# Other waves of token lists, and a re-drawn order, in a two-layer attention and expert kernel

## The chip, the cores and the metric

One core of a Trainium2 chip runs the whole program. The metric is the device time of one execution in microseconds; of several runs the median is taken. The engines are named as in the profile: PE is TensorE (PEld its weight loads), DVE is VectorE, ACT is ScalarE, POOL is GpSimd and SP is SyncE, whose queue issues most of the DMAs.

## What is computed

16 sequences of 256 tokens of 128 numbers (4096 tokens, all float32) pass two layers. Each layer is an attention, then a mixture of eight experts, each followed by a layer norm of input plus output:

```
x = layernorm(x + attention0(rmsnorm(x)))      # 16 heads of 64, softmax over 256 keys
x = layernorm(x + shared(x) + sum of the 2 best of 8 experts, by their softmax weight)   # hidden 256
x = layernorm(x + attention1(x))               # see below
x = layernorm(x + sum of the 2 best of 8 experts, by weight)                             # hidden 512
```

The experts' gelu is exact. The second attention has 16 heads of 8 and goes, as the reference writes it, over the heads of one token ("bnhd,bngd->bnhg"): each token has a 16 by 16 table of scores of its own, so it is elementwise work, not a matrix product over tokens.

## The kernel before, in words

**Tiling.** Tokens lie in 8 groups of 512, each four chunks of 128 tokens (one per partition). A unit of layer 0's attention is one sequence and two heads: 128 units, numbered in the order in which `attention0` (L662) takes them. For a unit, `scores` (L557) makes four products into PSUM, `softmax` (L528) takes the maximum on DVE (L533), the exponential with its sum on ACT (L539), the reciprocal on DVE (L550) and the scaling on POOL (L554); three units later `turn` (L579) transposes the result on PE and `attended` (L592) multiplies it with the values. `projected` (L502) and `values` (L520) make q, k and v ahead of their units, `project` (L617) the output of a half group, `summed` (L632) the residual and the norm.

**Experts by lists.** Apart from the last 256 tokens (second half of group 7), which go through all experts densely (`sequence` L1564, `dense` L1497), tokens go by lists. The parts are groups 0 to 6 and the first half of group 7. A *wave* is a set of parts that are routed together; `WAVES` (L33) names them for each layer:

```
WAVES = (((0, 1), (2, 3), (4, 5), (6, 7)), ((0, 1, 2, 3), (4, 5), (6, 7)))
NTS = [[2 * c + 7 for c in cs] for cs in CS]
```

A wave with C chunks has 2C token-expert pairs of chunks; as each expert's list is filled up to whole tiles of 128 rows, up to 2C+7 tiles are needed, and that many are always worked (L119). The steps of a wave: `logits` (L723) and `route` (L794, with `chosen` L747) on DVE with one small product on PE (L812 to L814) find each token's two places; `send` (L891) scatters the tokens into a list in DRAM, one indirect DMA on POOL for each chunk and choice (L900); `lists` (L964) works through the tiles in fours: loads of rows (L1009) and of each tile's expert weights (L1030, L1034, L1043), a turn on PE (L1055), first products (L1093), gelu on ACT (L1066, L1072), second products (L1113) and a store (L1131). Then `gathered` (L915) fetches each chunk's two results with indirect DMAs on POOL (L929) and adds them on DVE (L943). Only one wave at a time holds the lists; a wave of layer 1 that is not the last can give way to one of layer 0. In layer 0 the wave also passes `shared` (L1148), the expert that all tokens use, and it may add to a token only when that has been sent (L1187).

Between the layers, `middle` (L1392) takes each part on its own through norm, `attention1` (L1308) and the logits of layer 1. For each chunk `chunk1` (L1196) makes products of q and k on DVE (L1211), sums them (L1215), subtracts the maximum (L1240, POOL or DVE), takes the exponential (L1249), multiplies with v (L1287, POOL or DVE) and sums over keys (L1262, DVE). A branch in it, `heads_by_pe` (L1266), can make that last sum with products on PE, if by the planner's clocks PE will be idle for `SUMS` us.

**What sets the order.** No order is written down. While the program is built, `everything` (L318) repeatedly picks, of all strands (generators such as those above), the one whose next step can start first by a table of costs (the calls of `work`), moved by a favour and a rank for its kind (`KEYS`, L147; `PACE` L184 ranks the heads by half group). The instructions are put out in the order of these choices, and each engine runs its queue strictly in that order. Which of DVE, ACT and POOL makes a copy, a norm or a product is also chosen there (`copied` L258, `COPY`, `FAVOUR`). So new keys or costs change the order on every engine and the engine of many instructions.

Of the kernel before, what the change touches and what calls it, by code (L numbers as in the profile page):

```python
# [9 lines left out]
FP = mybir.dt.float32  # L10
# [5 lines left out]
P = 128  # L16
D = 128
NTOK = 16 * 256
GT = 512
NG = NTOK // GT  # L20
NC = GT // P
# [10 lines left out]
PARTS = [(g, 0, NC) for g in range(LAST)] + [(LAST, 0, NC // 2)]  # L32
WAVES = (((0, 1), (2, 3), (4, 5), (6, 7)), ((0, 1, 2, 3), (4, 5), (6, 7)))  # L33
I32 = mybir.dt.int32
# [3 lines left out]
def two_layers(  # L38
# [23 lines left out]
    nc = tc.nc  # L62
# [9 lines left out]
    ps_t = ctx.enter_context(tc.tile_pool(name="ps_t", bufs=2, space=PSUM))  # L72
# [37 lines left out]
    ident = const.tile([P, P], FP, tag="ident", name="ident")  # L110
    make_identity(nc, ident)
    mhalf = const.tile([P, NC], FP, tag="mhalf", name="mhalf")
    nc.gpsimd.memset(mhalf, -0.5)
# [20 lines left out]
    def cleared(layer, w):  # L134
# [12 lines left out]
    KEYS = {  # L147
        "copy qk": (-0.47, 0.098),
        "copy v": (-1.837, 0.311),
        "copy p": (-0.447, 0.289),  # L150
        "copy o": (-1.827, 0.05),
        "softmax": (-0.929, 0.15),
        "softmax 2": (-1.083, 0.3),
        "summed": (-2, 0.423),
        "normalised": (0.064, 0.401),
        "heads": (-0.036, 0.211),
        "w route": (0.209, 0.074),
        "w send": (-1.218, 0.245),
        "w shared": (-0.01, 0.358),
        "w loads": (-0.331, 0.017),  # L160
        "w turns 0": (-1.333, 0.096),
        "w turns 1": (0.218, 0.164),
        "w firsts 0": (-1.281, 0.243),
        "w firsts 1": (-0.641, 0.323),
        "w gelu": (-0.628, -0.115),
        "w seconds 0": (-0.513, 0.357),
        "w seconds 1": (0.844, 0.265),
        "w stored": (0.739, 0.057),
        "w gathered 0": (0.711, 0.093),
        "w gathered 1": (-0.147, -0.105),  # L170
        "w qkv": (0.126, -0.312),
        "w attention1": (0.364, 0.299),
        "w attention1 2": (1.784, 0.157),
        "w sums": (0.147, 0.241),
        "w normed": (-1.691, 0.205),
        "d loads": (-0.333, 0.978),
        "d route": (0.685, 0.221),
        "d firsts": (-0.122, -0.8),
        "d gelu": (-1.017, 0.988),
        "d seconds": (-0.245, -0.179),  # L180
        "d added": (-0.775, 1.421),
        "d normed": (0.891, 0.233),
    }
    PACE = [-0.064, 2, 0.528, -1.037, -1.955, -0.986, 0.284, 1.781]  # L184
    PACE += [1.065, 0.72, 1.611, 1.611, 1.069, 1.069, 1.469, 1.415]
    now = [0]
    COPY = -0.0
    SUMS = 14.742
    FAVOUR = -0.033
    SWITCH, SWITCH_BACK = 0.42, 0.949  # L190
    window, unit = [0, 0.0, 1.0], [P]
# [3 lines left out]
    end = {}  # L195
# [184 lines left out]
    def normed(y, o, tag, at):  # L380
# [9 lines left out]
        at = work("DVE", 0.43 * n, at)  # L390
        r, at = yield from powered(mv[:, :, 1], 1.0, 1e-5, tag, at)
# [10 lines left out]
        nc.gpsimd.tensor_scalar(nb, nb, -1.0, 1.0, ALU.mult, ALU.mult)  # L402
        at = work("POOL", 0.5, at)
        for c in range(n):
# [32 lines left out]
    def prepared():  # L437
# [22 lines left out]
        nc.gpsimd.memset(clear, 0.0)  # L460
        end["prepared"] = work("POOL", 9.0)

# [199 lines left out]
    def attention0():  # L662
        yield from projected(0, 0, wq_s, "q", qT)
        yield from projected(0, 0, wk_s, "k", kT)
        for c in range(NC):
            yield from values(0, 0, c)
        clears = [(0, 0), (0, 1), (1, 0), (0, 2), (1, 1), (0, 3), (1, 2)]
        for u in range(len(UNITS) + LAG):
# [4 lines left out]
            if g < NG:  # L673
# [27 lines left out]
                if i == 1 and 0 < g < LAST:  # L701
                    yield from values(g, 0, 3)
                yield from scores(u)
            if u >= LAG:
                yield from attended(u - LAG)
# [41 lines left out]
    def chosen(r, lg, layer, C, at):  # L747
# [22 lines left out]
        rs = small([P, C], "rs")  # L770
# [22 lines left out]

    def route(r, lg, layer, C, NT, at):  # L794
# [69 lines left out]
        if layer == 0:  # L864
# [331 lines left out]
    def chunk1(w, c, o, qv, kv, at, sums):  # L1196
# [462 lines left out]
```

## Time and profile before

| what | us |
|---|---|
| median of 3 runs (1244.42 to 1253.15) | 1245.04 |
| the profiled execution, as timed | 1250.27 |
| its span, first to last instruction | 1248.6 |
| PE busy | 1104.1 |
| DVE busy | 878.0 |
| ACT busy | 736.9 |
| POOL busy | 680.5 |

The span is cut here at four moments: the first scores (16.4), the issue of the last scores of layer 0's attention (860.5), the logits of layer 1's last wave (about 1100) and the last product of its list (1218). Up to 860 the heads of layer 0's attention run with the lists of three waves of layer 0 among them; behind it come layer 0's last wave, the dense half group and all lists of layer 1. A row of the busy time by stage gives, for each engine, the busy us and the number of instructions in brackets, then the clock granted to PE as a share of full speed, the DMA engines' mean busy share and GB/s. A row of a group gives line, engine, operation, tiles written and read, count, busy us, mean ns of one, and the engine's idle time just before them with what ended it. Float32 products are counted as two passes each.

### The profile page before, as it was taken

The page shows a single profiled execution, that of the slowest core. Times are in us where ns is not written, and L with a number is a line of the kernel's source. Part 1 is how long each engine was busy: PE and PEld are TensorE (multiplying, and loading weights), DVE is VectorE, ACT ScalarE, POOL GpSimd, SP SyncE. Part 2 cuts the span into 40 slices and gives each one's busy share as a digit, 9 for nine tenths or more (in the row PEclk, how much of TensorE's full clock was granted, in tenths as well). Part 3 has the DMA queues.
Part 4 walks back from the last instruction along what each step waited for, and adds up shares of the span by engine and source line. Part 5 has one row for each costly group of instructions (what it writes and reads, how often), then busy time and mean ns, then how long its engine had stood idle before and what let it go on. Part 6 is the DMA issues. An engine that isn't in the chain of part 4 may idle for free.

```text
span 1248.6 us, 22246 instructions
## 1 busy us (share of the span) xinstructions
PE 1104.1 (88%) x7175; PEld 795.3 (64%) x7175; DVE 878.0 (70%) x1748; ACT 736.9 (59%) x2086; POOL 680.5 (54%) x1059
## 2 busy tenths in 40 slices
PE   7999999979999999888999778998577998887985
PEld 3566665647665566656665456765455887887885
DVE  3766677634268897298789988779888779784433
ACT  5656566546757866477666567665346556544443
POOL 4434344372186647333765653485758827557654
PEclk9999999989999999789999889998768999888998
DMA  9800000033310003133000304213526879677981
GB/s 267 246 1 1 2 2 1 1 119 102 102 35 6 1 1 96 40 94 98 28 8 1 100 28 137 73 31 103 174 83 190 271 217 287 198 212 215 263 250 57
DMA packets 181527, 129.23 MB, mean 104 GB/s; under 512 B 12442, under 2 KB 165795, under 8 KB 181411
## 3 DMA queue, kind: packets, MB, share of 16 engines
q1 hardware_dynamic: 173730, 112.06, 30.4%
q0 software_dynamic: 7680, 15.74, 4.0%
q8 instruction: 58, 0.95, 0.3%
q14 instruction: 59, 0.48, 0.1%
HBM read 95.64 MB, written 32.11 MB: 102 GB/s over the span
## 4 chain that ended last, share of the span: by engine, by line
PE 49%; DVE 21%; POOL 14%; ACT 6%; issue 5%; DMA 4%; SPq 0%; ACTq 0%; POOLq 0%; DVEq 0%
PE s L570 8%; PE po L608 7%; POOL rows L900 7%; PE t L587 7%; PE ph L1093 3%; PE pv L524 3%; PE po_e L1113 3%; DVE qk_prod L1211 3%; PE pq L506 3%; PE pk L506 3%; PE py L625 3%; DMA y<-outs,r_pi 3%; DVE o L1262 3%; DVE sc L1215 2%; ACT pr L539 2%
## 5 line engine op out<-in xcount | busy, mean ns | idle before, releaser
L554 POOL TENSOR_SCALAR pr<-pr,rs 128x256 f32<-128x256 f32 x512 | 254.9, 515 | 329.4 <-DVE rs L550 237.7
L539 ACT ACTIVATE pr<-s,nm 128x256 f32<-128x256 f32 x512 | 235.6, 476 | 18.3 <-DVE nm L533 15.7
L533 DVE TENSOR_REDUCE nm<-s 128x4 f32<-128x1024 f32 x128 | 155.6, 1218 | 71.4 <-PE s L570 70.6
L1093 PE MATMUL ph<-xqT,wa 128*128 128x128 f32 x1000 | 139.1, 296 | 22.7 <-ACT h L1072 7.0
L587 PE MATMUL t<-ident,pr 128*128 128x128 f32 x1024 | 144.3, 282 | 6.7 <-POOL pr L554 4.6
L929 POOL DMA_INDIRECT y<-outs,r_pi x120 | 122.2, 1018 | 51.3 <-issue 23.4
L900 POOL DMA_INDIRECT rows<-x,r_pi x120 | 131.9, 1099 | 33.2 <-issue 20.8
L1093 PEld LDWEIGHTS ph<-xqT,wa 128*128 128x128 f32 x1000 | 129.6, 206 | 30.8 <-ACT h L1072 11.5
L608 PE MATMUL po<-pT,v 128*64 128x256 f32 x1024 | 142.4, 394 | 7.7 <-DVE kT L266 2.4
L587 PEld LDWEIGHTS t<-ident,pr 128*128 128x128 f32 x1024 | 112.9, 143 | 52.3 <-POOL pr L554 29.6
L570 PEld LDWEIGHTS s<-kT,qT 64*128 64x128 f32 x896 | 77.1, 186 | 85.2 <-issue 72.9
L570 PE MATMUL s<-kT,qT 64*128 64x256 f32 x896 | 127.0, 402 | 0.8 <-ACT pr L539 0.8
L266 DVE COPY pT<-t 128x512 f32<-128x512 f32 x146 | 95.4, 684 | 43.0 <-PE t L587 42.7
L268 ACT COPY oT<-po 128x256 f32<-128x256 f32 x103 | 38.3, 372 | 128.2 <-PE po L608 128.2
L608 PEld LDWEIGHTS po<-pT,v 128*64 128x64 f32 x1024 | 64.0, 136 | 67.4 <-issue 18.7
L539 ACT ACTIVATION_READ_ACCUMULATOR pr<-s,nm 128x1 f32 x512 | 106.2, 207 | 0.0
L1287 POOL TENSOR_TENSOR av_prod<-sc,qkv 128x1024 f32<-128x1024 f32 x28 | 70.8, 2535 | 60.6 <-ACT sc L1249 49.7
L1211 DVE TENSOR_TENSOR qk_prod<-qkv 128x1024 f32<-128x1024 f32 x64 | 82.3, 1286 | 10.1 <-ACT qkv L268 9.9
L268 ACT COPY pT<-t 128x512 f32<-128x512 f32 x110 | 61.2, 589 | 38.3 <-PE t L587 38.1
L1262 DVE TENSOR_REDUCE o<-av_prod 128x64 f32<-128x1024 f32 x64 | 76.1, 1205 | 6.0 <-POOL av_prod L1287 5.7
L1215 DVE TENSOR_REDUCE sc<-qk_prod 128x128 f32<-128x1024 f32 x64 | 78.1, 1220 | 2.2
L1113 PE MATMUL po_e<-wb,h 128*128 128x128 f32 x648 | 77.9, 279 | 1.7 <-ACT h L1066 1.4
(229 smaller groups left out, 1966.9 us busy)
## 6 DMA issues: line engine op xcount, KB each, us to landing
wa<-in_w_dram SPq DMA_DIRECT2D x176, 128.0 KB
wa<-in_w_dram SPq DMA_DIRECT2D x81, 256.0 KB
wb<-in_w_dram SPq DMA_DIRECT2D x81, 256.0 KB
xq<-rows SPq DMA_DIRECT2D x37, 256.0 KB
outs<-yq SPq DMA_DIRECT2D x37, 256.0 KB
rows<-clear SPq DMA_DIRECT2D x4, 1472.0 KB
rows<-clear SPq DMA_DIRECT2D x1, 2496.0 KB
rows<-clear SPq DMA_DIRECT2D x2, 1216.0 KB
```

The costliest lines, as they stand in the source:

```text
L533: nc.vector.tensor_reduce(nm[u], s, AX.X, ALU.max, negate=True)
L539: nc.scalar.activation(pr[u][:, i, :], s[:, i, :], AF.Exp, bias=nm[u][:, i : i + 1], accum_out=su[u][:, i : i + 1],)
L554: nc.gpsimd.tensor_scalar(pr[u][:, i, :], pr[u][:, i, :], rs[:, i : i + 1], 1.0, ALU.mult, ALU.mult)
L570: nc.tensor.matmul(sc[u][:, j, qc, :], q[part, ts(qc, P)], k[part, :], start=True, stop=True,)
L587: nc.tensor.transpose(t[:, kc, ts(qc, P)], pr[u][:, 2 * j + qc, ts(kc, P)], ident)
L608: nc.tensor.matmul(po[j * DH : (j + 1) * DH, :], vs[g, p // 4, 2 * b + kc][:, ts(h, DH)], pT[u][j][:, kc, :], start=(kc == 0), stop=(kc == 1),
L900: i = nc.gpsimd.indirect_dma_start(out=rows[layer][w][:, :], out_offset=bass.IndirectOffsetOnAxis(ap=r.pos[:, k, c : c + 1], axis=0), in_= ...
L929: nc.gpsimd.indirect_dma_start(out=y, out_offset=None, in_=outs[layer][w][:, :], in_offset=bass.IndirectOffsetOnAxis(ap=r.pos[:, k, c0 + c ...
L1093: nc.tensor.matmul(ph[:, q - q0, c, :], was[i, q][0][:, c, :], xTs[i][0][:, q, :], start=True, stop=True)
L1113: nc.tensor.matmul(po[:, q, :], hs[i, q][0][:, c, :], wbs[i, q][0][:, c, :], start=(c == 0), stop=(c == nh - 1))
L1211: nc.vector.tensor_tensor(m, q3[:, ts(j, HALF)].unsqueeze(2).to_broadcast(full), k3.unsqueeze(1).to_broadcast(full), ALU.mult)
L1262: nc.vector.tensor_reduce(o[:, c, ts(j, P // 2)], m.rearrange("p h d g -> p (h d) g"), AX.X, ALU.add)
```

## The change

The waves become 0 / 1 / 2, 3 / 4, 5 / 6 and half of 7 in layer 0, and 0 to 2 / 3 to 5 / 6 and half of 7 in layer 1. PE first transposes `ident` 28 times into a tile that nobody reads. In `attention0` the first four values products are put behind the first two units' scores (two behind each) and no longer ahead of them; the lists in DRAM are cleared in a new order, one more of them. All `KEYS`, `PACE`, `COPY`, `SUMS`, `FAVOUR` and the two `SWITCH` numbers are new, and some costs of the planner's table (not of the chip) are. Nothing else in the code differs.

```diff
-WAVES = (((0, 1), (2, 3), (4, 5), (6, 7)), ((0, 1, 2, 3), (4, 5), (6, 7)))
+WAVES = (((0,), (1,), (2, 3), (4, 5), (6, 7)), ((0, 1, 2), (3, 4, 5), (6, 7)))
...
     make_identity(nc, ident)
+
+    t = ps_t.tile([P, GT], FP, tag="t", name="t_busy")
+    for c in range(28):
+        nc.tensor.transpose(t[:, ts(c % NC, P)], ident, ident)
...
-        "copy qk": (-0.47, 0.098),
-        "copy v": (-1.837, 0.311),
+        "copy qk": (0.751, 0.355),
+        "copy v": (-0.105, 0.247),
...
-    PACE = [-0.064, 2, 0.528, -1.037, -1.955, -0.986, 0.284, 1.781]
-    PACE += [1.065, 0.72, 1.611, 1.611, 1.069, 1.069, 1.469, 1.415]
+    PACE = [-2, 0.239, 0.902, 0.46, -0.063, 0.882, 1.35, 1.473]
+    PACE += [1.91, 2, 2, 1.138, 0.3, 0.896, 1.503, 0.278]
     now = [0]
-    COPY = -0.0
-    SUMS = 14.742
-    FAVOUR = -0.033
-    SWITCH, SWITCH_BACK = 0.42, 0.949
+    COPY = 0.364
+    SUMS = 11.982
+    FAVOUR = 0.906
+    SWITCH, SWITCH_BACK = 1.155, 0.348
...
-        at = work("POOL", 0.5, at)
+        at = work("POOL", 0.4, at)
...
-        end["prepared"] = work("POOL", 9.0)
+        end["prepared"] = work("POOL", 4.0)
...
-        for c in range(NC):
-            yield from values(0, 0, c)
-        clears = [(0, 0), (0, 1), (1, 0), (0, 2), (1, 1), (0, 3), (1, 2)]
+        clears = [(0, 0), (0, 1), (0, 2), (1, 0), (0, 3), (1, 1), (0, 4), (1, 2)]
...
                 yield from scores(u)
+                if u < 2:
+                    for c in (2 * u, 2 * u + 1):
+                        yield from values(0, 0, c)
...
-            at = work("DVE", 1.0 + 0.03 * C, at)
+            at = work("DVE", 1.3 + 0.05 * C, at)
...
-        r.at = at = work("DVE", 2.3, at)
+        r.at = at = work("DVE", 2.6, at)
...
-            r.weighed = work("DVE", 1.8, at)
+            r.weighed = work("DVE", 2.1, at)
...
-            mine["rs"] = work("DVE", 0.6, at)
+            mine["rs"] = work("DVE", 0.7, at)
```

More of the change, by code (lines that the diff above doesn't have):

```diff
@@ L147, in two_layers @@
     KEYS = {
-        "copy qk": (-0.47, 0.098),
-        "copy v": (-1.837, 0.311),
[L150 to L182, printed above, removed]
-    }
-    PACE = [-0.064, 2, 0.528, -1.037, -1.955, -0.986, 0.284, 1.781]
-    PACE += [1.065, 0.72, 1.611, 1.611, 1.069, 1.069, 1.469, 1.415]
+        "copy qk": (0.751, 0.355),
+        "copy v": (-0.105, 0.247),
@@ new lines, in two_layers @@
+        "copy p": (0.001, 0.711),
+        "copy o": (-1.111, 0.398),
+        "softmax": (-1.575, 0.277),
+        "softmax 2": (0.342, 0.721),
+        "summed": (1.025, 0.224),
+        "normalised": (1.884, 0.322),
+        "heads": (-1.003, -0.214),
+        "w route": (-1.669, 0.073),
+        "w send": (-0.164, 0.164),
+        "w shared": (-1.579, 0.257),
+        "w loads": (0.256, 0.033),
+        "w turns 0": (0.513, 0.162),
+        "w turns 1": (0.251, 0.475),
+        "w firsts 0": (0.512, 0.321),
@@ new lines, in two_layers @@
+        "w firsts 1": (0.277, -0.114),
+        "w gelu": (-1.133, 0.343),
+        "w seconds 0": (1.219, 0.901),
+        "w seconds 1": (0.414, -0.246),
+        "w stored": (0.549, -0.273),
+        "w gathered 0": (1.405, 0.228),
+        "w gathered 1": (0.09, -0.54),
+        "w qkv": (0.428, 0.38),
+        "w attention1": (-1.481, -0.013),
+        "w attention1 2": (1.487, 0.229),
+        "w sums": (1.397, 0.194),
+        "w normed": (-0.46, 0.55),
+        "d loads": (-1.653, 0.921),
@@ L186, in two_layers @@
+        "d route": (-0.18, 0.818),
+        "d firsts": (-1.068, 0.307),
+        "d gelu": (0.575, 0.062),
+        "d seconds": (0.232, 0.311),
+        "d added": (-1.836, 0.618),
+        "d normed": (-1.302, 0.51),
+    }
+    PACE = [-2, 0.239, 0.902, 0.46, -0.063, 0.882, 1.35, 1.473]
+    PACE += [1.91, 2, 2, 1.138, 0.3, 0.896, 1.503, 0.278]
     now = [0]
-    COPY = -0.0
-    SUMS = 14.742
-    FAVOUR = -0.033
-    SWITCH, SWITCH_BACK = 0.42, 0.949
+    COPY = 0.364
+    SUMS = 11.982
```

## The prediction

> **What bounds the kernel now.** I read the page first, then the busy time by stage, then groups by line, then the timeline at both ends. TensorE carries the span: 1104.1 of 1248.6 us are busy, and the other engines are at 70% or less.
>
> ```profile
> span 1248.6 us, 22246 instructions
> PE 1104.1 (88%) x7175; PEld 795.3 (64%) x7175; DVE 878.0 (70%) x1748; ACT 736.9 (59%) x2086; POOL 680.5 (54%) x1059
> PEclk9999999989999999789999889998768999888998
> ```
>
> By stage (start, last scores issued, end of the stall behind them, logits of layer 1's last wave, end of its list, end) the 144 us without TensorE are not spread evenly. Columns are the stretch, its length, busy time by engine, granted clock, DMA share and GB/s:
>
> ```profile
> 0.00:16.40 16.40, 8.90 (x20) 3.53 (x20) 1.65 (x6) 6.76 (x16) 5.38 (x29) 1.00 0.88 273
> 16.40:860.50 844.10, 785.18 (x4998) 515.75 (x4997) 610.72 (x1117) 541.55 (x1706) 432.63 (x721) 0.97 0.19 55
> 860.50:967.00 106.50, 74.17 (x387) 55.13 (x387) 91.97 (x185) 54.32 (x127) 74.93 (x107) 0.76 0.50 152
> 967.00:1101.00 134.00, 115.49 (x855) 105.70 (x853) 107.78 (x209) 71.22 (x121) 75.07 (x86) 0.93 0.81 242
> 1101.00:1218.00 117.00, 102.57 (x807) 98.96 (x808) 56.29 (x192) 53.29 (x100) 77.40 (x96) 0.93 0.79 235
> 1218.00:1248.60 30.60, 17.77 (x120) 16.21 (x118) 9.56 (x41) 9.74 (x19) 15.05 (x21) 0.86 0.19 58
> ```
>
> While heads of layer 0's attention remain, 58.9 of 844.1 us are lost; behind the last scores 78 of 388. Inside the first stretch the loss sits in the three stages with layer 0's lists (10.4, 15.2 and 20.0 us, 45.6 together); the fourth line is the stage in which groups 6 and 7 pass layer 1's attention:
>
> ```profile
> 260.00:345.00 85.00, 74.61 (x491) 54.91 (x489) 25.38 (x50) 53.10 (x152) 30.34 (x60) 0.96 0.36 107
> 485.00:585.00 100.00, 84.78 (x505) 62.79 (x504) 62.97 (x115) 63.37 (x162) 42.75 (x64) 0.90 0.28 83
> 690.00:800.00 110.00, 89.96 (x596) 66.92 (x593) 92.58 (x163) 71.58 (x189) 52.55 (x78) 0.92 0.31 91
> 1003.00:1101.00 98.00, 82.92 (x598) 75.55 (x597) 84.00 (x153) 52.63 (x88) 47.60 (x56) 0.91 0.77 229
> ```
>
> The prices (busy us, mean ns; a float32 matmul is two of the counted passes):
>
> ```profile
> L1093 PE MATMUL ph<-xqT,wa 128*128 128x128 f32 x1000 | 139.1, 296 | 22.7 <-ACT h L1072 7.0 <-ACT h L1066 6.9 <-DVE xqT L266 2.3
> L1113 PE MATMUL po_e<-wb,h 128*128 128x128 f32 x648 | 77.9, 279 | 1.7 <-ACT h L1066 1.4 <-DVE d_lg L733 0.3
> L1055 PE MATMUL px<-ident,xq 128*128 128x128 f32 x169 | 27.9, 294 | 5.5 <-DMA xq<-rows 5.5
> L1249 ACT ACT_TABLE_LOAD x15 | 19.2, 1283 | 0.3
> ```
>
> And both ends. The first projection takes 2.08 us for two passes, where 112 passes take 58.7 us (1.05 for two). After the logits of layer 1's last wave at 1098.4 another 150 us follow, and TensorE has other work in most of them:
>
> ```profile
> 6.72 1.11 PE L489 MATMUL t_h<-ident,xn 128*128 128x128 f32 x4 [6.72 <-DVE xn L477]
> 8.61 2.08 PE L506 MATMUL pq<-hT,wq 128*128 128x512 f32 x2 [0.78 <-ACT hT L498]
> 1098.40 2.73 PE L729 MATMUL pl<-rw,xT 128*128 128x8 f32 x12
> 1221.29 1.08 POOL L929 DMA_INDIRECT y<-outs,r_pi  x1 [6.99 <-DMA outs<-yq]
> ```
>
> **The change, part by part.** The counts of the changed kernel are from its instruction queues as built.
>
> Work added. A list has 2C+7 tiles for C chunks, so layer 0 goes from 23+23+23+19 = 88 tiles to 15+15+23+23+19 = 95; layer 1 stays at 81 (39+23+19, then 31+31+19). A layer-0 tile is a turn (27.9/169 = 0.165 us), two first products (139.1/500 = 0.278 each) and two second ones ((77.9+45.8)/500 = 0.247): 1.22 us, seven are 8.5. One more route is 0.8. TensorE: +9.3 us, all on the path, as it is the bound. The seven tiles' 14 weight loads and the eighth clearing pass SP's queue in a stretch with DMA at 0.19: nothing, unless that cover goes.
>
> Work moved between engines by the new KEYS. VectorE does 45 instructions fewer (mostly copies of 0.69 us, 8 of its 36 products av_prod, 17 of its 24 subtractions): about -46 us. ScalarE takes most of the copies at 0.59 us plus eight more table loads (64 against 56): about +46. GpSimd gains 8 products of 2.54 and 17 subtractions of 0.63, less a little: +28. None becomes the engine with the most work.
>
> The table loads are worth weighing. The row has 1.283 us for one and 0.3 us of idle time before fifteen, so eight cost 10.3 us of ScalarE, beside TensorE for the most part. The Trainium skill (ScalarE: Activation LUTs, What ACT_TABLE_LOAD costs) adds a drain of about 1.38 us to each switch; by it the eight would be 21 us, and the forecast up to 11 us later if all stood on the path. The trace shows no such drain: at 1110.74 a load follows a copy that ended at 1110.71, and its exponential starts at 1112.03.
>
> The start. The 28 transposes of ident run cold from about 1.4 us, when ident is made; at 1.11/4 = 0.28 us each they take 7.8 us, to 9.2, if nothing speeds up, and t_h, ready at 6.72, waits 2.5 us. If the clock rises as it did between t_h and the values, they are done in time and the first q and k run at the usual pace: 2.08+1.50 becomes about 1.77, a gain of 1.8. I take the gain; bounds -1.8 and +2.5. Scores ahead of values moves 3.8 us of TensorE work behind work that is ready; TensorE had no wait there but 0.78 us, so nothing.
>
> Head sums. The built queues have no TensorE head sum, before or after (L1262 is 64 VectorE reductions in both); SUMS changes nothing: 0.
>
> What is moved ahead of the last scores. Before, 69 list tiles stand ahead of them in TensorE's queue; after, 107: layer 0's 76 and of layer 1's wave 0 the turns of all 31 tiles, the first products of 25 and the second of 20 (four each). That is 8.5 (the seven tiles) + 25x4x0.278 + 20x4x0.247 + 31x0.165 = 61.2, plus one more group through layer 1's attention (3.4 for qkv, 1.4 projection, 2.4 turns, 1.1 logits) and three routes, the added one among them, 2.4: 72 us. With the stalls of before kept, and the start's 1.8 gained, the last scores stand at 860.5 + 72 - 1.8 = 930.7; the mean price of a row is a little high for plain attention (eight units cost 39.6 by rows, 38.8 in the timeline), so 927. The stall in this stretch is unknown from both sides: 0 more if the tiles mix with heads, less by up to 45.6 if all list stalls go, more by 45.6x38/69 = 25.1 if each tile costs what it does now. I keep 58.9, as VectorE has less to do but there are five stages instead of three.
>
> Behind the last scores TensorE had 310 us (the last four stages' sum); 72 - 9.3 = 63 of them are gone, and counted leg by leg from the rows 242 are left (65 + 58 + 72 + 47). Four legs:
> - To the route of layer 1's wave 1 (rest of wave 0's list, last heads, shared expert, dense layer 0): TensorE 65; the like stretch of before needs 106.5 for 74. There 9.7 us are a wait for sent rows and 8.6 for a normalisation; after, the scatter is queued ahead of the products, so I take 78 (bounds 65 and 93).
> - To group 6's turn into layer 1's attention: TensorE 58, but GpSimd's queue holds 24 scatters (0.97+0.12 and the gap, 1.27 to 1.29 each in the timeline: 31), 20 gathers at 1.25 (25), a product 2.5, four normalisations at 1.5 (6), and starts 4 us after the route, with a landing and a norm behind: 72 (bounds 58 and 80).
> - Six chunks of layer 1's attention, to the logits: TensorE 72, VectorE 61. The stage of before at 1003 has them at 0.85 and 0.86 of the time, which gives 84 and 71: 80 (bounds 72 and 90).
> - The end, new in this form: dense is finished, wave 1's list too, so nothing of TensorE covers. Route to positions 11 (the VectorE rows from 1121.75 to 1131.5 and the exponential), 12 scatters and their landing with the load of xq 24 (15.4 + 2.7 + 5.4), the list of 19 tiles 45 (1173 to 1218 before), and 31 from its last product to the end (1218 to 1248.6): 111. Behind the scatters in GpSimd's queue stand 24 gathers of groups 3 to 5 (30 us), which end before the list does. Before, this stretch was 150 with 120 of TensorE inside. Bounds 105 and 118.
>
> Sum: 927 + 78 + 72 + 80 + 111 = 1268 of span. The profiled execution took 1250.27 for 1248.6, 1.7 more, and lies 5.2 above the median of 1245.04: 1268 + 1.7 - 5.2 = 1264.5, so 1264, or 1.5% slower. In short, the front gains 67 us; the tail goes from 388 to 341.
>
> **Rivals.**
> - Faster: the stalls of the list stages go. Place: 260 to the last scores; price: up to 45.6 us, 1219. For it: octets of before where lists mix with heads lose 3 to 5%, and the smaller waves mix more. Against: five stages, and 104 to 112 still has VectorE (83 by rows) over TensorE (80). It decides once 32 of the 45.6 us go (1264 - 32 = 1232).
> - The same: GpSimd is not last in the second leg and VectorE not in the third, so TensorE's 58 and 72 stand: 22 us less, 1242. For it: both engines have waits to give; against: the 0.85 of before's stage.
> - Much slower: a list tile stalls as now, 45.6x107/69, so 25 more: 1289. For it: the clock falls to 0.76 where TensorE waits, and every new stage has a shared expert with its own wait.
> - It doesn't do what it says: true of the head sums, and worth 0.
>
> **How the numbers follow.** The forecast has 0.40, much slower 0.18, the same 0.25, faster 0.17. A measurement of this kernel can tell about 1% from no change (1232.6 to 1257.5). So slower 0.58, same 0.25, faster 0.17; the range leaves out most of the faster case and the worst of the slower: 1236 to 1290. The likeliest case alone has 1258 to 1278.
>
> **What would show it.** Right: last scores near 927; a wait of TensorE of 20 us or more ahead of the last list's first turn, with GpSimd's twelve scatters in it; 30 us without TensorE at the end; 1113 of TensorE plus the 28 transposes. Wrong: last scores before 900, or the logits of the last wave before 1125; a late TensorE head sum would void the count.

## The result and the profile after

| | before | changed |
|---|---|---|
| median, 15 runs each, us | 1248.05 | 1254.25 |
| lowest to highest | 1244.21 to 1256.12 | 1252.80 to 1260.82 |
| profiled execution, as timed, and its span | 1250.27, 1248.6 | 1255.12, 1253.3 |

The ratio is 1.0050, with a 95% interval of 1.0029 to 1.0072: slower by half a per cent, where 1.5% was forecast. The time lies inside the range of the forecast, but below the 1258 to 1278 of its likeliest case and in the band that it called no change, to which it gave 0.25. The median of before from three runs, on which the forecast stood, was 3 us below that from fifteen.

The page of the changed kernel, its span, busy times and granted clock in 40 slices:

```profile
span 1253.3 us, 22522 instructions
PE 1101.7 (88%) x7272; PEld 797.9 (64%) x7272; DVE 842.2 (67%) x1703; ACT 779.1 (62%) x2172; POOL 711.1 (57%) x1085
PEclk9999999999999998999999789999999878999596
```

TensorE does 97 passes more than before and is busy 2.4 us less. The busy time by stage, cut at the moments that the prediction named: first scores, issue of the last scores, route of layer 1's wave 1, turn of group 6, logits of the last wave, then first turn and last product of its list:

```profile
0.00:12.10 12.10, 9.88 (x38) 7.15 (x38) 0.86 (x2) 5.70 (x16) 2.11 (x8) 1.00 0.77 238
12.10:927.25 915.15, 853.27 (x5512) 575.06 (x5512) 652.74 (x1210) 624.36 (x1860) 513.69 (x830) 0.98 0.26 78
927.25:996.10 68.85, 62.52 (x427) 51.63 (x426) 47.47 (x146) 37.60 (x78) 44.22 (x60) 0.98 0.68 200
996.10:1077.40 81.30, 63.60 (x396) 57.13 (x397) 49.32 (x141) 40.89 (x95) 62.80 (x90) 0.83 0.52 155
1077.40:1153.30 75.90, 66.62 (x531) 62.00 (x529) 65.64 (x90) 43.72 (x75) 34.19 (x26) 0.98 0.66 196
1153.30:1185.46 32.16, 6.01 (x50) 5.73 (x50) 8.10 (x36) 4.56 (x7) 18.07 (x29) 0.66 0.66 202
1185.46:1225.70 40.24, 39.80 (x323) 39.14 (x323) 11.94 (x52) 19.25 (x36) 21.96 (x26) 0.93 0.79 235
1225.70:1253.30 27.60, 0.01 (x1) 0.00 (x0) 6.14 (x26) 3.00 (x7) 14.02 (x18) 0.56 0.18 50
```

The last scores come 66.8 us later than before (927.25 against 860.5). Behind them 326.0 us follow, where 388.1 did, so 62 of the 67 us come back. TensorE idles for 64.1 us ahead of the last scores (66.4 before) and 87.5 behind (78.1 before). The largest wait is new: in the sixth row it works 6 of 32 us. On its timeline, with the two ends:

```profile
1.43 5.87 PE L115 MATMUL t_busy<-ident 128*128 128x128 f32 x28 [1.43 <-POOL ident masks.py:199]
9.29 1.12 PE L510 MATMUL pq<-hT,wq 128*128 128x512 f32 x2 [0.78 <-ACT hT L502]
...
1160.11 0.35 PE L819 MATMUL pc<-r_scratch,ones 128*128 128x8 f32 x2
1185.46 1.97 PE L1060 MATMUL px<-ident,xq 128*128 128x128 f32 x8 [25.00 <-DMA xq<-rows]
1187.25 5.71 PE L1098 MATMUL ph<-xqT,wa 128*128 128x128 f32 x32
...
1222.87 2.84 PE L1118 MATMUL po_e<-wb,h 128*128 128x128 f32 x24
```

Between the last route's products at 1160 and the turn at 1185 lie the positions, twelve scatters on GpSimd and their landing; behind the last product it is the gathers:

```profile
1163.45 1.11 POOL L905 DMA_INDIRECT rows<-x,r_pi  x1 [11.86 <-DVE r_scratch L860]
1177.58 0.97 POOL L905 DMA_INDIRECT rows<-x,r_pi  x1 [0.19 <-issue]
1229.12 1.07 POOL L934 DMA_INDIRECT y<-outs,r_pi  x1 [9.45 <-DMA outs<-yq]
```

The prices of before, in the same groups (line numbers are 4 or 5 higher):

```profile
L1098 PE MATMUL ph<-xqT,wa 128*128 128x128 f32 x1028 | 142.6, 294 | 30.3 <-ACT yq L272 11.8 <-ACT h L1071 5.8 <-ACT h L1077 5.7
L1118 PE MATMUL po_e<-wb,h 128*128 128x128 f32 x648 | 76.3, 276 | 2.6 <-ACT h L1071 2.6
L1060 PE MATMUL px<-ident,xq 128*128 128x128 f32 x176 | 29.3, 299 | 32.8 <-DMA xq<-rows 32.0 <-ACT v L272 0.5 <-DVE pT L270 0.3
L1254 ACT ACT_TABLE_LOAD x14 | 18.0, 1283 | 0.2
```

### The profile page after: what moved, and what is told of

Its sections match the earlier page's. It is cut to its first block, busy times and chain, and to the rows that moved or that the text cites. A ratio compares the mean times of both kernels' runs of the same rounds, so it can differ in the third digit from the quotient of the medians.

```text
span 1253.3 us, 22522 instructions
## 1 busy us (share of the span) xinstructions
PE 1101.7 (88%) x7272; PEld 797.9 (64%) x7272; DVE 842.2 (67%) x1703; ACT 779.1 (62%) x2172; POOL 711.1 (57%) x1085
## 4 chain that ended last, share of the span: by engine, by line
PE 63%; DVE 12%; POOL 9%; ACT 7%; issue 4%; DMA 3%; SPq 1%; ACTq 0%; POOLq 0%; DVEq 0%
PE s L574 10%; PE po L612 9%; PE t L591 8%; PE po_e L1118 5%; PE ph L1098 4%; PE pv L528 4%; PE pq L510 4%; POOL rows L905 3%; PE pk L510 3%; PE py L629 3%; DMA y<-outs,r_pi 2%; ACT pr L543 2%; DVE o L1267 2%; PE ph_d L1528 2%; POOL av_prod L1292 2%
## 5 line engine op out<-in xcount | busy, mean ns | idle before, releaser
L543 ACT ACTIVATE pr<-s,nm 128x256 f32<-128x256 f32 x512 | 235.8, 476 | 27.5 <-DVE nm L537 25.9
L1098 PE MATMUL ph<-xqT,wa 128*128 128x128 f32 x1028 | 142.6, 294 | 30.3 <-ACT yq L272 11.8
L1098 PEld LDWEIGHTS ph<-xqT,wa 128*128 128x128 f32 x1028 | 131.6, 204 | 40.7 <-ACT yq L272 12.6
L934 POOL DMA_INDIRECT y<-outs,r_pi x120 | 117.5, 979 | 61.1 <-issue 22.4
L1292 POOL TENSOR_TENSOR av_prod<-sc,qkv 128x1024 f32<-128x1024 f32 x36 | 87.8, 2455 | 31.2 <-ACT sc L1254 31.1
L272 ACT COPY oT<-po 128x256 f32<-128x256 f32 x106 | 39.3, 371 | 105.4 <-PE po L612 105.3
L270 DVE COPY pT<-t 128x512 f32<-128x512 f32 x130 | 85.2, 685 | 23.9 <-PE t L591 23.7
L948 DVE SCALAR_TENSOR_TENSOR x<-y,r_gate,x 128x128 f32<-128x128 f32 x120 | 46.5, 393 | 72.5 <-DMA y<-outs,r_pi 71.1
L272 ACT COPY pT<-t 128x512 f32<-128x512 f32 x126 | 70.6, 591 | 24.3 <-PE t L591 24.0
L1220 DVE TENSOR_REDUCE sc<-qk_prod 128x128 f32<-128x1024 f32 x64 | 78.1, 1220 | 2.2
```

The source lines that it names most:

```text
L272: nc.scalar.copy(o, i)
L543: nc.scalar.activation(pr[u][:, i, :], s[:, i, :], AF.Exp, bias=nm[u][:, i : i + 1], accum_out=su[u][:, i : i + 1],)
L934: nc.gpsimd.indirect_dma_start(out=y, out_offset=None, in_=outs[layer][w][:, :], in_offset=bass.IndirectOffsetOnAxis(ap=r.pos[:, k, c0 + c ...
L1098: nc.tensor.matmul(ph[:, q - q0, c, :], was[i, q][0][:, c, :], xTs[i][0][:, q, :], start=True, stop=True)
L1292: (nc.gpsimd if e == "POOL" else nc.vector).tensor_tensor(m, sc1[:, ts(j, HALF)].unsqueeze(2).to_broadcast(full), v3.unsqueeze(1).to_broad ...
```

## The experiments

Each is compared with runs of the kernel before on its own chip. The time itself is given too; e13 to e15 ran on a chip where the kernel before took 5% longer, and there only the ratio says something.

### The start: e1, e13, e17

e1 takes the transposes out of the changed kernel, e13 and e17 put them, and nothing else, into the kernel before. e1:

```diff
-    for c in range(28):
-        nc.tensor.transpose(t[:, ts(c % NC, P)], ident, ident)
```

> The changed kernel without its 28 transposes of ident; the order of all else is the same. Theory of the prediction: they warm the clock, and the scores after the fourth stand 2.0 us earlier in the changed kernel (32.57 against 34.57 for the sixth), so without them the start loses about 2 us, and as heads run back to back behind it the end does too: 2 us longer than the changed kernel, 1256. Rival (given back later): a wait of the list stages absorbs it, 1254. Rival (work): TensorE has 5.9 us less to do, 1248.

> The kernel before with the 28 transposes of ident alone; the order of all else is the same. In e1 the changed kernel lost about 2.7 us without them (ratio 1.0072 against 1.0050). If the start is worth that wherever it stands: 1246 to 1247, ratio 0.998. If a wait of the list stages absorbs it: 1249, ratio 1.000. If the transposes delay t_h (7.3 against 6.7 us): 1249 to 1250.

> The kernel of e13 beside e16 on one chip, since e13 ran where the kernel before itself took 1310.9. If the gain of 0.3% holds: 1244 to 1247, below both kernels. If it was noise: 1248 to 1250.

e1: 1258.16, ratio 1.0072 (1.0044 to 1.0101) against the changed kernel's 1.0050. e13: 1308.27 where before took 1310.85, ratio 0.9970 (0.9947 to 0.9994). e17: 1246.50, ratio 0.9977 (0.9954 to 0.9999). The first products without and with them, e1 and then e17:

```profile
8.99 2.08 PE L507 MATMUL pq<-hT,wq 128*128 128x512 f32 x2 [0.78 <-ACT hT L499]
34.55 1.14 PE L571 MATMUL s<-kT,qT 64*128 64x256 f32 x8
```

```profile
1.43 4.64 PE L115 MATMUL t_busy<-ident 128*128 128x128 f32 x28 [1.43 <-POOL ident masks.py:199]
8.48 1.13 PE L510 MATMUL pq<-hT,wq 128*128 128x512 f32 x2 [0.78 <-ACT hT L502]
33.15 1.13 PE L574 MATMUL s<-kT,qT 64*128 64x256 f32 x8
```

The first product takes 1.13 instead of 2.08. The sixth scores stand at 34.57 before, 34.55 in e1 (all of the change but the transposes), 33.15 and 32.91 in e17 and e13 (transposes alone), 32.57 in the changed kernel. So the transposes are worth 1.4 to 2.0 us there, and the rest of the change, with the values behind the scores, nothing by itself. By the medians the end moves as far or farther (0.2 to 0.3%). The intervals are too wide to say by how much: that of e1 overlaps the changed kernel's, and that of e17 ends at 0.9999. The kernel of e13 and e17 is the one version here that is faster than both kernels, by 0.2 to 0.3% of before.

### Waves or keys: e2, e3, e8, e12

e2 is the changed kernel with the old waves (and the old order of clearing), e3 the kernel before with the new ones; e8 and e12 are the changed kernel with only one layer's waves new.

```diff
-WAVES = (((0,), (1,), (2, 3), (4, 5), (6, 7)), ((0, 1, 2), (3, 4, 5), (6, 7)))
+WAVES = (((0, 1), (2, 3), (4, 5), (6, 7)), ((0, 1, 2, 3), (4, 5), (6, 7)))
```

> The changed kernel with the waves of before; keys, costs, start and values are those of the change. TensorE has 8.5 us less to do than in the changed kernel, and 59 us less ahead of the last scores (817 against 876 by rows). Cover theory (what stands behind the last scores is set by chains of scatters, lists and gathers that TensorE only partly fills; what the waves move ahead comes back as waits): last scores near 868, the tail 293 of TensorE and 75 to 90 without it, 1236 to 1251. Work theory (the waves cost their tiles and nothing else): 1245. Theory that keys and not waves make the difference: as the changed kernel, 1254.

> The kernel before with the new waves (and the order of clearing that they need); keys and costs are those of before. By rows 895 us of TensorE stand ahead of the last scores and 217 behind them, against 876 (with the transposes) and 242 in the changed kernel. Cover theory: last scores near 950, the tail has 217 of TensorE and 95 to 115 without it, 1262 to 1282, slower than the changed kernel. Work theory: 1248 + 9, 1257. Theory that keys and not waves make the difference: as before, 1248.

> The changed kernel with layer 0's waves as before and layer 1's as changed. It tells which half of the old waves made e2 99 us longer than the changed kernel. If layer 0's (two groups in the first wave, under keys made for one): near 1353. If layer 1's (four groups in its first wave): near 1254 - 8. Both in part: 1280 to 1320.

> The changed kernel with layer 0's waves as changed and layer 1's as before: the fourth of the four pairs (both new 1254, both old 1353, layer 1's alone 1340). If layer 0's waves and the keys belong together and layer 1's are neutral: 1254 + 0 to 10. If each layer's waves carry a part: 1290 to 1320. By TensorE's order 61 us less stand ahead of the last scores than in the changed kernel, so last scores near 866 and a tail of 304 with 75 to 90 of waits: 1245 to 1260.

| | last scores | last route | TensorE idle behind last scores | time |
|---|---|---|---|---|
| before | 861 | 1126 | 78 | 1248.05 |
| changed | 928 | 1160 | 88 | 1254.25 |
| e2: old waves, new keys | 901 | 1250 | 146 | 1353.40, ratio 1.0841 (1.0804 to 1.0879) |
| e3: new waves, old keys | 973 | 1219 | 117 | 1325.38, ratio 1.0604 (1.0566 to 1.0642) |
| e8: only layer 1's waves new | 917 | 1243 | 141 | 1339.61, one run |
| e12: only layer 0's waves new | 864 | 1167 | 136 | 1314.71, one run |

The sums by TensorE's cover missed, e3 by 43, e12 by 55 and e2 by 100 us; e12 lies in the range in which each layer's waves carry a part, and e8 between that range and the 1353 of layer 0's waves alone, nearer to the latter. A part of the change alone costs 5 to 8%, all of it half a per cent: waves and keys have no effect of their own that could be added. What TensorE waits for behind the last scores of e2, and of e3 (us in total, times, longest):

```profile
PE px L1060 <- DMA xq<-rows: 40.1, 4, 27.8
PE t_x L419 <- ACT x L409: 23.5, 7, 8.8
```

```profile
PE px L1055 <- DMA xq<-rows: 37.1, 3, 22.2
PE ph L1093 <- DVE d_lg L733: 17.2, 1, 17.2
```

Rows of a list not there, norms not done, a product held by a far strand: the same kinds of waits as in the tuned pair, at other places and longer. What they cost can't be told from the wave sizes; it stands in the queues as built.

### Filling the last wait: e4, e11, e16, e18

In e4 six, in e11 four of the eight dense experts of layer 1 may start only when the last wave is routed:

```diff
+                    late = layer == 1 and ORDER[1].index(e) >= 2
-                    yield (lambda: max(at, HS.free(), there[layer, e][2] if (layer, e) in there else INF)), "PE", "s"
+                    yield (lambda: INF if late and routed1[-1].listed == INF else max(at, HS.free(), ...)), "PE", "s"
```

> The changed kernel, but six of the eight dense experts of layer 1 (24 us of TensorE) may start only when the last wave is routed. They then fill the 25 us in which TensorE waits for the last list's rows, and the second wave's list runs in their old place from 1053 to 1077. Cover theory: the turn of group 6 is no longer behind dense products (4 us), the stretch to the logits of the last wave falls from 76 to VectorE's 66 (8 to 10), and the wait of 25 us is under 5: 1238 to 1243. Rival (chain): GpSimd's and the lists' chain sets the end whatever TensorE does in the gaps: 1250 to 1254. Rival (late dense): the dense products delay the last list's turn by their excess over the wait, and the end by 0 to 5 us: 1254 to 1259.

> As e4, but four experts late in place of six. In e4 group 6's turn came 5 us earlier counted from the last scores, VectorE kept the stretch behind it at the old end, and six experts delayed the last list's turn from 25 to 31 us after the route. If that reading is right, four experts (16 us) no longer delay it: 1249 to 1254, 3 to 7 less than e4. If late dense products cost by themselves (their gelu, weights or adds): 1255 to 1258 as e4.

e4: 1256.61, ratio 1.0062 (1.0043 to 1.0082). e11: 1252.59, ratio 1.0032 (1.0018 to 1.0046). The stages of e4 from the route of wave 1 on (cut at group 6's turn, the end of the last logits and the list's turn), and of e11 from group 6's turn to the issue of its last logits:

```profile
998.40:1075.50 77.10, 58.38 (x395) 53.34 (x396) 45.22 (x125) 39.93 (x93) 60.54 (x87) 0.85 0.69 205
1075.50:1157.50 82.00, 59.41 (x431) 52.85 (x430) 63.96 (x93) 35.25 (x63) 43.08 (x34) 0.85 0.50 150
1157.50:1194.60 37.10, 26.54 (x150) 23.48 (x151) 16.14 (x73) 10.44 (x19) 27.12 (x41) 0.78 0.66 195
```

```profile
1072.43:1148.69 76.26, 64.49 (x485) 58.75 (x485) 61.36 (x87) 41.03 (x74) 36.22 (x27) 0.93 0.59 174
```

In e4 the wait is filled (26.5 of 37 us). Group 6 is turned 4 us sooner behind the route, but the half of group 7, which the changed kernel turns with it, comes at 1081.2, later than there. The stage behind the turn takes 82.0 where the changed kernel needs 76.5 to the same point, with 7 us less of TensorE in it, and the list's turn comes 37 us behind the logits, not 32. (The profiled execution of e4 is its slowest, 5.4 us above its median, so a part of this may be that execution's.) In e11 group 6 is turned 6.7 us sooner, the stage takes 76.3 (75.9 in the changed kernel), the list's turn comes 33.8 us behind the logits, and 2 us of the gain are left, within the intervals. So a free TensorE didn't shorten that stage, and late experts delay the list. My 10 to 15 us for e4 were wrong; its time lies in the range of the rival on late dense products (1254 to 1259), and the later list turn that this rival named is in the trace.

e16 and e18 put idle transposes, 200 and 230, into the wait of the changed kernel:

```diff
+        if w == len(WAVES[1]) - 1:
+            t = ps_t.tile([P, GT], FP, tag="t", name="t_wait")
+            for c in range(200):
+                nc.tensor.transpose(t[:, ts(c % NC, P)], ident, ident)
```

> The changed kernel with 200 more transposes of ident behind the last route's products, where TensorE waits 25 us; the order of all else is the same. In the changed kernel the last list's first 28 passes run at half pace (0.213 us apart until 1191.0, 0.11 behind that), 5.6 us that would take 2.9. If that is the wait's price: 2.5 to 3 us less, 1251 to 1252. Rival (TensorE isn't what the list's start waits for: gelu, copies and weights are): 0 to 1 us less. Rival (the transposes run into the turn): 0 to 3 us more.

> As e16 with 230 transposes in place of 200. In e16 they ended 3.3 us ahead of the turn, and the clock fell anyway for the first 32 products (5.5 us), so e16 told nothing of a warm start. 230 at 0.11 us end where the rows arrive. If the clock is the price of the wait: the turn and the first products take 3.9 and not 5.6 us, 2 to 3 us less than the changed kernel, 1251 to 1252. Rival (the start waits for copies, gelu and weights): 1253 to 1255. Rival (the transposes run past the rows' arrival): up to 2 us more.

e16: 1253.91, ratio 1.0033 (1.0013 to 1.0054). e18: 1255.92, ratio 1.0060 (1.0038 to 1.0083). The turn and first products of e16, then of e18:

```profile
1158.81 22.03 PE L1422 MATMUL t_wait<-ident 128*128 128x128 f32 x200
1184.13 0.66 PE L1060 MATMUL px<-ident,xq 128*128 128x128 f32 x4 [3.29 <-DMA xq<-rows]
1185.51 5.50 PE L1098 MATMUL ph<-xqT,wa 128*128 128x128 f32 x32
```

```profile
1159.12 25.30 PE L1422 MATMUL t_wait<-ident 128*128 128x128 f32 x230
1185.42 0.66 PE L1060 MATMUL px<-ident,xq 128*128 128x128 f32 x4 [0.99 <-DMA xq<-rows]
1186.76 3.94 PE L1098 MATMUL ph<-xqT,wa 128*128 128x128 f32 x32
```

After 3.3 us of idling the turn is fast, but the products behind it are slow; after 1.0 us they take 3.94 instead of 5.71. That is the 1.8 us that a warm clock gives. The list is 39.2 us long against 40.2, and its turn comes 23.2 us behind the first scatter against 22.0, though the transposes had ended 1.0 us before it. Both ratios lie around the changed kernel's 1.0050 with overlapping intervals, so a gain of 1 to 2 us is neither shown nor excluded; the median of e18, whose start was warm, has no sign of the 2 to 3 us that it expected.

### Fewer or more tiles at the end: e5, e6

The last wave of layer 1 is split, in the changed kernel (e5) and in the kernel before (e6); seven tiles more.

```diff
-... ((0, 1, 2), (3, 4, 5), (6, 7)))
+... ((0, 1, 2), (3, 4, 5), (6,), (7,)))
```

> The changed kernel with layer 1's last wave in two: group 6 (15 list tiles) and half of group 7 (11) in place of 19, seven tiles more. The order up to the logits of group 6 is the same. End theory (what follows the last wave's logits is a chain that TensorE doesn't cover: route 10, scatters 1.27 each, landing and load 6.6, list 2.12 a tile, 3.4 to the first gather, gathers 1.25 each, 9.3 to the end): group 6 routed about 1149, its rows by 1167, its list until 1199, the last list 23 more, then 3.4 + 5 + 9.3, so a span of 1240, 13 less than the changed kernel: 1241. Rival (work): seven tiles are 15.9 us of TensorE, all on the path: 1270. Rival (GpSimd): its queue takes 24 gathers of groups 3 to 5 ahead of the new scatters, 30 us: 1254 to 1260.

> The kernel before with the same split of layer 1's last wave. There the dense half group still stands ahead of the last list and behind it, so TensorE has cover. End theory: the uncovered part is smaller (list 45 us and 30.6 behind it, with 17.8 us of TensorE in that), so the split gains less than in the changed kernel: 15.9 us more work against up to 17 + 10 us of shorter list and gathers, 1238 to 1250. Rival (work): 1264. Rival (the changed kernel's end isn't special): the same gain as there.

e5: 1273.23, ratio 1.0190 (1.0175 to 1.0205). e6: 1272.17, ratio 1.0192 (1.0172 to 1.0212). My end theory missed by 32 us in e5 (1241) and by 22 or more in e6 (1238 to 1250). The work rival's numbers (1270 and 1264) are nearer, with e5 3 and e6 8 us above them. By the ratios the split costs 1.4% in the changed kernel and 1.9% in the one before. Between the two last lists of e5, on TensorE and on SP's queue:

```profile
1195.95 3.78 PE L1118 MATMUL po_e<-wb,h 128*128 128x128 f32 x32
1211.07 2.00 PE L1060 MATMUL px<-ident,xq 128*128 128x128 f32 x8 [11.33 <-DMA xq<-rows]
```

```profile
1198.60 7.66 SPq L1039 DMA_DIRECT2D wa<-in_w_dram  x9
1206.36 1.78 SPq L1014 DMA_DIRECT2D xq<-rows  x3
```

Its rows had been sent by 1172, but one list at a time is worked, and of the next the first nine weights are loaded ahead of its rows: 11.3 us at a change of lists with nothing else to do. In e6 dense products fill most of that change (TensorE waits 1.4 us for the rows) and it loses more, so these 11.3 us don't explain both; what does is open.

### VectorE's stage: e7, e9, e10

e7 sets SUMS to 0, so that ten head sums use TensorE; e9 raises FAVOUR once the heads are over; e10 is e9 with four late experts.

```diff
-    SUMS = 11.982
+    SUMS = 0.0
...
-            if max(clk["DVE"], at) + 1.25 + FAVOUR < max(clk["POOL"], at) + 2.35:
+            if max(clk["DVE"], at) + 1.25 + (4.0 if "over" in end else FAVOUR) < max(clk["POOL"], at) + 2.35:
```

> The changed kernel with SUMS at 0: ten of the late head sums go to TensorE, four in the dense half group and six in group 6, 1.2 us of VectorE less for each and sixteen small products more on TensorE. Chain theory (the stretch from group 6's turn to the last logits, 76 us, is set by VectorE, busy 65.6): 6 to 8 us less in it, 1246 to 1248. Rival (TensorE sets it, busy 66.6): longer by 6 x 1 to 2 us, 1260 to 1266. Rival (GpSimd's products are last): no change, 1252 to 1256.

> The changed kernel with one number of the planner raised once the heads are over (FAVOUR 4 in place of 0.906 from there on), so that four products av_prod of the last chunks go to GpSimd in place of VectorE (24 on VectorE in place of 28). VectorE theory (from group 6's turn to the last logits VectorE is back to back from 1080 to 1145, TensorE's 66.6 are beside it): four products of 1.94 us leave it, the stretch of 76 falls by 5 to 8: 1246 to 1249. Rival (TensorE sets the stretch): 1253 to 1255. Rival (a product takes GpSimd 2.5 us and each chunk's sum waits for it): 1256 to 1260.

> As e9, and four of the eight dense experts of layer 1 (16 us of TensorE) wait until the last wave is routed, so that they fill part of the 25 us wait. VectorE theory: the gain of e9, and group 6's turn 3 to 5 us earlier as in e4, and the dense products, 16 us, end before the last list's rows are there: 1240 to 1246. Rival (late dense delays the last list as in e4, where its turn came 31 us after the route and not 25): 1250 to 1256. Rival (TensorE sets the stretch): 1248 to 1250, by the earlier turn alone.

e7: 1282.39, ratio 1.0255 (1.0237 to 1.0273). e9: 1267.68, ratio 1.0144 (1.0123 to 1.0165). e10: 1259.41, ratio 1.0084 (1.0066 to 1.0101). The group of e7 (passes: shortest, median, longest ns), and its two stages, from the route of wave 1 to group 6's turn and on to the last logits:

```profile
L1274 PE MATMUL o_sums<-av_prod,ident x320: 269/289/406, 1022.5 to 1153.6; 128*128 128x64 f32 x160
```

```profile
997.73:1095.20 97.47, 84.26 (x548) 77.14 (x548) 44.49 (x137) 42.20 (x98) 61.29 (x90) 0.86 0.45 136
1095.20:1182.04 86.84, 83.30 (x700) 79.08 (x698) 60.26 (x91) 39.78 (x65) 29.93 (x23) 1.00 0.54 162
```

Ten sums cost TensorE 39.9 us (1141.6 busy against 1101.7), 4.0 each where the planner's table has 1.95, and spare VectorE 1.2 each. The two stages grow from 81.3 and 75.9 to 97.5 and 86.8. So TensorE has little room there; the rival that had it as the limit was right in kind, but its 1260 to 1266 were too low. In e9 VectorE has two products less in its stage (the second one, from the turn at 1083.31), and the stage is longer:

```profile
1083.31:1163.09 79.78, 71.42 (x572) 66.64 (x570) 62.05 (x88) 45.64 (x78) 39.65 (x27) 0.98 0.64 189
```

VectorE's 62 of 79.8 us say that it isn't the limit alone; the changed order put 5 us more of TensorE into the stage. It also moved group 6's turn 5.0 us back behind the route and made the list 2.6 us longer, and e9's time lies above all three readings that were given for it (at most 1260). So does e10's (at most 1256): its stage takes 76.4 us with 61.9 of TensorE and 60.8 of VectorE, and its list's turn comes 35.3 us behind the logits. With less of TensorE (e4), of VectorE (e9) or of both (e10, e11) the stage was not shorter, and with more of TensorE (e7) it was longer. That the two are balanced and each works behind the other fits this, but isn't shown: every one of these runs changed the order of other work too, and GpSimd's part (34 us busy in that stage) was not tested alone.

### Layer 0's last wave in two: e14, e15

The chain from layer 0's last wave to the last route was to be shortened by giving group 6 a wave of its own (and moving a scratch column so that two chunks fit).

```diff
-WAVES = (((0,), (1,), (2, 3), (4, 5), (6, 7)), ...
+WAVES = (((0,), (1,), (2, 3), (4, 5), (6,), (7,)), ...
```

> The changed kernel with layer 0's last wave in two (group 6, half of group 7; seven tiles more, 8.5 us; a scratch column of the route moved so that two chunks fit). Chain theory (the end hangs on the chain from layer 0's last wave through group 6's attention to the last route, 1160): group 6 can pass ahead of the last scores, the last route comes near 1060 to 1100, and the end near TensorE's own 1110 + 80 to 100: 1200 to 1225. Rival (order): the keys were made for other waves, as in e2, e3, e8 and e12, and the planner puts the new wave late: 1270 to 1350.

> The kernel before with the same split of layer 0's last wave. Chain theory: the last route, 1126 before, comes 30 to 60 us earlier and the end 10 to 40 us: 1210 to 1240. Rival (order): 1270 to 1350.

e14: 1385.61 and e15: 1372.42, one run each, where before took 1310.85 on that chip: 1.057 and 1.047. In e14 group 6 is routed at 842, but its list is turned at 991, behind the last scores (892), and the last route comes at 1256. The chain was not shortened, so the theory was not tested; the times, by their ratios, are those of the rival on the order, as in the four runs above.

## Why the prediction was right and wrong, point by point

- **Start**: -1.8 forecast, -2.0 measured. Right.
- **Last scores**: 927 forecast, 927.25 measured. TensorE's work ahead of them grew by 69.1 us, 5.9 of it the transposes, and its idle time fell by 2.3; I had 66.5 in all. The trace has the 107 list tiles and three more routes ahead of them: right. The sum is closer than its parts: work apart from the transposes grew by 63.2, less than the 66.5, the list stalls by 3.0, for which I had nothing, and these cancel.
- **List stalls**: 58.9 kept, 61.9 measured, with five stages in place of three. This decided both the faster rival (32 of 45.6 us had to go) and the much slower one (25 more): neither happened.
- **Leg to the route of wave 1**: 78 forecast, 68.9 measured. I carried the waits of before over (9.7 for sent rows, 8.6 for a norm). TensorE idled only 6.3: the twelve scatters (929.5 to 951.4) ran beside what was left of a list and the last heads, and the shared expert came at 957, when the rows were sent. My lower bound, 65, was the better guide; this is read from the trace, no run changed it alone. That this leg's -9.1 and the next one's +9.3 cancel in the sum is luck.
- **Leg to group 6's turn**: 72 forecast, 81.3 measured. GpSimd was last, as said (62.8 of 81.3 busy, scatters from 1002.5 to 1042.7, gathers behind). The 24 scatters, with a product and two norms between them, took 40 us, for which I had 36.5 (31 + 2.5 + 3), as some took 2.0 us and not 0.97; they began 6.4 us behind the route, not 4, and dense products stood ahead of the turn for 2 us more: 8 of the 9 us. In e1, e16 and e18, with the same order from the first scores up to there, the leg took 80.3, 79.9 and 78.6.
- **Leg to the last logits**: 80 forecast (0.85 of the time busy), 75.9 measured, with TensorE at 0.88 and VectorE at 0.86. Right in kind: the shares are those of the row of before, but TensorE had 66.6 to do and not 72.
- **The end, the step that failed**: "the list of 19 tiles 45 (1173 to 1218 before), and 31 from its last product to the end", 111 in all. It measured 100.0: 10.1 to the first scatter (11 forecast), 22.0 to the turn (24), 40.2 for the list, 27.6 behind. So 8 of the 11 us are in the last two, where the rows of before held other work. The 45 hold 17 passes of the dense half group (2.0 us) and 3.6 us of waits, where the changed kernel has 0.4. The list of before, and most of its dense passes:

```profile
1172.92:1217.86 44.94, 41.36 (x340) 40.44 (x341) 17.08 (x68) 20.17 (x40) 25.75 (x33) 0.96 0.89 267
1173.41 1.95 PE L1536 MATMUL po_d<-wd,h_d 128*128 128x128 f32 x16
```

In the 31 the gathers end as far behind the last product as after the change (18.4 and 18.3 us), and 17.8 us of dense products run beside them. What is longer is the rest, 12.4 us against 9.3: before, one more pair of chunks, the dense half group's, goes through a norm and an output there, and that output waits for one store more. The last outputs of before, then of the changed kernel:

```profile
1241.93 0.88 ACT L405 ACTIVATE ye<-x,n_nb,n_r 128x128 f32<-128x128 f32 x2 [2.27 <-DMA out_dram<-ye]
1244.65 0.88 ACT L405 ACTIVATE ye<-x,n_nb,n_r 128x128 f32<-128x128 f32 x2 [1.84 <-DMA out_dram<-ye]
```

```profile
1249.58 0.88 ACT L409 ACTIVATE ye<-x,n_nb,n_r 128x128 f32<-128x128 f32 x2 [2.30 <-DMA out_dram<-ye]
```

Twelve kernels with that list have it alone on TensorE:

| | scatters to turn | list of 19 tiles | last product to end |
|---|---|---|---|
| changed | 22.0 | 40.2 | 27.6 |
| e1, e7, e9 | 22.3, 21.4, 21.8 | 39.6, 40.3, 42.8 | 27.6, 27.6, 27.7 |
| e4, e10, e11 | 25.1, 22.4, 24.5 | 38.0, 39.3, 40.7 | 27.7, 27.7, 27.8 |
| e16, e18 | 22.2, 23.2 | 39.6, 39.2 | 27.7, 27.6 |
| e2, e3, e8 | 21.7, 24.6, 23.0 | 47.0, 43.0, 39.4 | 27.7, 28.0, 27.7 |

Of these only e2's list is as long as I had it; the last stretch is the same everywhere. e17, in the order of before, has 44.8 and 30.7 as before. On the slower chip e14's list took 57.7 with 15.0 us of waits in it and e15's 40.6, and their last stretches 27.5 and 28.0.
- **Span to median**: I took 5.2 off for the profiled run against three runs, and added 1.7. In the changed kernel the profiled run lies 0.9 above the median. Legs -14.7 (-9.1 + 9.3 - 4.1 - 11.0, and 0.2 at the last scores) and this +4.4 make 1264.5 into 1254. The base of three runs is not why the change came out smaller, as it lowers the forecast and the time before alike: span against span the forecast was +19.4, the measurement +4.7.
- **The rival within 1%** (1242, GpSimd and VectorE not last): its number is nearly as near as mine (12 us off against 10), its mechanism didn't occur: GpSimd was last in its leg, and the next leg took 75.9 for 66.6 of TensorE.
- **Engines**: DVE -35.8 (forecast -46), ACT +42.2 (+46), POOL +30.6 (+28): right in kind; none became the bound. There are 64 table loads of 1283 ns, as built. The Trainium skill's drain (ScalarE: Activation LUTs, What ACT_TABLE_LOAD costs) doesn't appear after the change either: the group at L1254 has 0.2 us of idle time before fourteen loads.
- **TensorE's total**: 1113 and the transposes forecast, 1101.7 measured. Passes are quicker than in the rows of before: 282 fell to 279 ns for 1024 turns, 349 to 323 for 120 products of the shared expert. That fewer of them are cold, and that this is all of the difference, is not shown.
- **Head sums**: none built, none in the trace; e7 shows that they would have cost 4 us each.

So the mechanism was the one forecast: the front gains work, the tail gives most of it back in time, and a wait that nothing covers is new. Behind the last scores I had 242 us of TensorE and 99 without it; it was 238.6 and 87.5, and 10 of the missing 12 us of waits are in the end. The size was a third of the forecast because the end was priced by a stretch with other work in it: with 100 in its place the sum gives 8 us more than before, 0.7%. Open is whether the chain through layer 0's last wave decides the tail (e14 and e15 didn't shorten it), and what share of the half per cent belongs to waves and what to keys: e2, e3, e8 and e12 show that the question has no answer by parts.

## What to carry to other kernels

Before a stretch of the old profile is used as the price of a stage, take out of it what doesn't belong to the stage: count its passes and its waits, not its length. Where an order is searched together with the sizes that it orders, cost the built queues as one; half of such a change is another kernel. And a wait that nothing covers isn't yet a gain: three ways to fill the 25 us here (dense work, idle transposes, a smaller last list) gave 2 us at most, within the intervals, or cost up to 19. What the list waits for, the scatters and their landing, became no shorter by any of them.

## What the runs showed of the hardware

- The clock of TensorE steps, and the time to the step varies. The 128-wide float32 passes at the start and in the last list begin 0.213 us apart and then go on 0.11 us apart. The last slow one starts 5.2 us behind the first (changed kernel, start), 3.0 and 2.8 (e13 and e17, the same transposes) and 5.6 (changed kernel, 1185.5 to 1191). The Trainium skill (TensorE: Matmul & The Clock Gate, What's actually happening) has about 3.4 us of sustained work, counted in a free-running window; the runs lie around that, from 2.8 to 5.6.
- 3.3 us of idling were enough for the clock to fall in e16: the granted clock is 0.5 from 1185.41 to 1188.83, beginning 1.3 us after work had begun again. 1.0 us were not in e18.
- Chips differ: the kernel before took 1310.85 (17 runs, granted clock 0.92) on the chip of e13 to e15 and 1247 to 1251 on the others (0.94).
- A change of lists cost 11.3 us of TensorE where nothing else was ready (e5): the next list's rows are issued at 1206.36, behind nine loads of its weights that take SP's queue 7.66 us.
